# A gated recurrent layer on one core: h @ wh moved into a bf16 bank of three exact pieces

## The chip, the cores and the metric

The kernel runs on one core of a Trainium2 chip. The metric is the device time of one execution in microseconds. Every kernel is launched once per execution; a profiled execution also leaves a trace, from which all durations below are read.

## The reference

Eight sequences of 512 steps with 512 features each. The state h (8 x 512) starts at `cond_1024`. What matters of the reference:

```
def step(h, x_t):
    fused = sigmoid(concat([x_t, h]) @ w_W + w_b)
    r, z = split(fused, 2)                      # hidden_state, output_state
    memory = x_t @ wx_W + wx_b + r * (h @ wh_W + wh_b)
    h_new = z * h + (1 - z) * tanh(memory)
    return h_new, h_new
out = x + all h_new
```

Each step needs the state of the step before it. The x products (`x_t @ ...`) do not, so they can be done ahead of time. Everything is float32.

## The kernel before, in words

**Layout.** The 512 hidden units stand as 4 quarters (`k`) of 128 partitions. The state is the stationary operand of every matmul: a quarter of h, with 8 batch columns among 32 (the other 24 columns are zero; four consecutive steps, a *group* of `GS = 4`, use different rows of the same bank). The weights are streamed. Four output strips `j` of 32 PSUM partitions run side by side, so one "group of matmuls" for a quarter `k` is four matmuls with the same number of columns. The units are further cut into half A (quarters 0 and 1) and half B (2 and 3).

**Banks.** In the kernel before, each group of steps has three PSUM banks: A with 192 columns (h @ wh, z and r of half A), B with 128 (r and h @ wh of half B) and C with 64 (z of half B). `ORDER` is the order of the matmul groups in a step; the digit is the quarter of h. After them comes one portion of the x side. All matmuls are f32.

**A step after the matmuls.** DVE transposes pieces of the banks back to the layout of the state in 32 x 32 blocks (`turn_r`, `turn_h`, `turn_z`). ScalarE takes the sigmoids. A `tensor_tensor_scan` (`memory`) makes r * (h @ wh) + x part, ScalarE takes tanh, another scan (`update`) makes the new state, separately for the two quarters of each half. ScalarE copies the state into slot 0 of the state tile; GpSimd adds x for the output. The order on DVE is written out by hand: r, h, z of A, memory scans of A, r and h of B, first state scan of A, z of B, second state scan of A, memory and state scans of B.

**The x side.** The products for two groups of steps are made together from seven instead of eight half-size products (`products`, with `weight_sum` and `x_sum` making sums of weights and of x); DVE and ScalarE combine them over eight steps into the tile `xs`, from which `spread` fills the banks and `turn_x` transposes the x part of the memory.

**Order of the work.** `tc.manual_schedule()` leaves every engine's instructions in program order. PSUM, state and work tiles are double buffered or more. SP loads the weights and one chunk of x per 16 steps and stores one chunk of output per 16 steps.

**Lines.** In the profile of before, L194 is every matmul (`mm`), L224 every activation (`act`), L390 every scan, L406 the transposes of r and z, L422 that of h, L262 that of x, L558 the output adds, L534 and L495 two of the combinations of x products, L257 the `spread` copies, L232 the `seed` copy of the bias.

Of the kernel before, what the change touches and what calls it, by code (L numbers as in the profile page):

```python
# [16 lines left out]
B = 8  # L17
HU = 64

DVE_FILL = 23
IDLE = 3
LAST = 4
SYNC = mybir.DependencyInfo(mybir.DependencyClass.Sync, mybir.DependencyReason.DATA)

ORDER = "A0 B0 A1 A2 A3 B1 B2 B3 C0 C1 C2 C3"

FIRST = "A0 x A1 x A2 x A3 B0 B1 B2 B3 C0 C1 C2 C3"

BANKS = {"A": 192, "B": 128, "C": 64}

HALF = 192

WIDE = 384

SUMS = ((2,), (2,), (2, 1), (2, 1), (1,), (1, 3), (3,), (3, 3))

Q01, Q23 = slice(0, 64), slice(64, 128)

COLS = slice(64, 448)

XP = {"A": slice(0, 192), "X": slice(192, 320), "C": slice(320, 384), "B": slice(384, 512)}
# [3 lines left out]
def tile_cond_rnn_residual(  # L47
# [7 lines left out]
    wb3_d: bass.AP,  # L55
# [4 lines left out]

# [13 lines left out]

# [56 lines left out]

    wa = const.tile([P, NQ, NQ, 192], F32, name="wa")
    for k in range(NQ):
        nc.sync.dma_start(out=wa[:, k], in_=wa_d[k])
    wb = const.tile([P, NQ, NQ, 192], F32, name="wb")
    nc.sync.dma_start(out=wb[:, :3], in_=wb_d)
    nc.sync.dma_start(out=wb[:, 3], in_=wb3_d)

    def wh(bank, k, j):
        return wa[:, k, j] if bank == "A" else wb[:, k, j, {"C": slice(0, 64), "B": slice(64, 192)}[bank]]  # L140
# [3 lines left out]
    def pair(n, name, rows, slots):  # L144

        return const.tile([P, 2, rows, slots], F32, name=name).rearrange("p c n s -> p n c s")

    NH = 2 * GS  # L150
    hT = [[pair(n, f"hT{n}{i}", 32, 3) for i in range(NH)] for n in "AB"]

    md0 = [[pair(n, f"md0{n}{i}", 32, 2) for i in range(2)] for n in "AB"]
    md1 = [[pair(n, f"md1{n}{i}", 32, 2) for i in range(2)] for n in "AB"]
    hd0 = [[pair(n, f"hd0{n}{i}", B, 3) for i in range(2)] for n in "AB"]
# [11 lines left out]
    for n, t_ in enumerate(hd0[0] + hd0[1] + md0[0] + md0[1] + hT[0] + hT[1]):  # L167
        (nc.vector if n < DVE_FILL else nc.gpsimd).memset(t_, 0.0)
    for t_ in hd0[0] + hd0[1]:
        nc.gpsimd.memset(t_[:, :, :, 1], -1.0)  # L170
    idle = const.tile([P, IDLE], F32, name="idle")

    tw = [const.tile([P, 2, 2, WIDE], F32, name=f"tw{n}") for n in range(4)]
    sx = [[const.tile([P, 2, GS * B], F32, name=f"sx{n}{q}") for q in range(2)] for n in range(4)]
    step_bias = const.tile([P, HALF], F32, name="stepbias")
    xs = [const.tile([P, 512], F32, name=f"xs{n}") for n in range(2)]
    u2 = const.tile([P, WIDE], F32, name="u2")
    u3 = const.tile([P, WIDE], F32, name="u3")
    both = const.tile([P, WIDE], F32, name="both")

    def state(hf, i, slot=2):

        s = i % GS
        return hT[hf][i % NH][:, B * s : B * s + B, :, slot]

    ctx.enter_context(tc.manual_schedule())
    banks = [
        {n: psum.tile([P, w], F32, name=f"{n}{q}") for n, w in BANKS.items()}
        for q in range(2)
    ]  # L190
    xps = [psum.tile([P, 512], F32, name=f"xp{q}") for q in range(2)]

    def mm(out_, lhsT, rhs, start=False):
        nc.tensor.matmul(  # L194
            out_, lhsT, rhs, start=start, stop=False, skip_group_check=True
        )


    for t_ in list(banks[0].values()) + list(banks[1].values()):
# [10 lines left out]
    for t_ in xs:  # L210
        for c_ in (slice(0, 64), slice(448, 512)):
            nc.gpsimd.tensor_copy(t_[:, c_], bias[:, c_])
    for hf in range(2):
        for slot in (0, 2):
            nc.vector.tensor_copy(
                state(hf, 0, slot), hin[:, 2 * hf : 2 * hf + 2].rearrange("p c b -> p b c")
            )


# [9 lines left out]

    def seed(g):  # L230

        nc.scalar.copy(xps[g % 2][:, COLS], bias[:, COLS])  # L232

    def prefill(g):

        c, t0 = divmod(g * GS, TC)
        for k in range(NQ):
            for j in range(NQ):
                mm(
                    xps[g % 2][32 * j : 32 * j + 32, 64:448],  # L240
                    x_of(c, k, t0, GS),
                    wx[:, k, j, :],
                )
            yield

    def prefill_two():
        yield from prefill(2)
        yield from prefill(3)

    def source(g):  # L250

        return xs[g % 2] if g else xps[0]

    def spread(g, names):

        for n in names:
            nc.scalar.copy(banks[g % 2][n], source(g)[:, XP[n]])  # L257

    def turn_x(g, e):

        c0 = XP["X"].start + 32 * e
        nc.vector.transpose(md1[e // 2][g % 2][:, :, e % 2, 1], source(g)[:, c0 : c0 + 32])  # L262

    def wx_of(kh, nh):
        return wx[:, 2 * kh : 2 * kh + 2, 2 * nh : 2 * nh + 2]

    def x_half(o, n, kh):

        return x_of(o // 2, slice(2 * kh, 2 * kh + 2), 8 * (o % 2) + GS * n, GS)

    def weight_sum(n, k=slice(0, 2), j=slice(0, 2)):

        a, b = [
            (wx_of(0, 1), wx_of(0, 0)),
            (wx_of(1, 1), tw[0]),
            (wx_of(1, 1), wx_of(0, 1)),
            (wx_of(1, 0), tw[1]),
        ][n]
        at = (slice(0, P), k, j)
        nc.vector.tensor_tensor(tw[n][at], a[at], b[at], ALU.subtract)  # L280

    def x_sum(o, n):

        t_ = [q[o % 2] for q in sx]
        a, b, op = [
            (x_half(o, 1, 0), x_half(o, 1, 1), ALU.add),
            (t_[0], x_half(o, 0, 0), ALU.subtract),
            (x_half(o, 0, 0), x_half(o, 1, 0), ALU.subtract),
            (x_half(o, 0, 1), t_[1], ALU.subtract),
        ][n]  # L290
        nc.gpsimd.tensor_tensor(t_[n], a, b, op)

    def products(o):

        t_ = [q[o % 2] for q in sx]
        p1 = (0, x_half(o, 0, 0), wx_of(0, 0))
        p2 = (0, x_half(o, 0, 1), wx_of(1, 0))
        p3 = (0, t_[3], wx_of(1, 1))
        p4 = (1, x_half(o, 1, 1), tw[3])
        p6 = (0, t_[1], tw[1])  # L300
        p7 = (1, t_[2], tw[2])

        def pair(left, right, k, c0=0, c1=WIDE):
            for j in range(NQ):
                bank, lhs, rhs = left if j < 2 else right
                mm(
                    xps[bank][32 * j : 32 * j + 32, COLS.start + c0 : COLS.start + c1],
                    lhs[:, k],
                    rhs[:, k, j % 2, c0:c1],
                    start=right is p7 and k == 0 and j >= 2,  # L310
                )

        def shared(k):
            for j in range(NQ):
                c0 = HALF * (1 - j // 2)
                mm(
                    xps[j // 2][32 * j : 32 * j + 32, COLS.start : COLS.start + HALF],
                    t_[0][:, k],
                    tw[0][:, k, j % 2, c0 : c0 + HALF],
                )  # L320

        pair(p1, p7, 0)
        yield
        pair(p1, p7, 1)
        yield
        pair(p2, p6, 0)
        yield
        pair(p2, p6, 1)
        yield
        pair(p4, p3, 0, 0, 288)  # L330
        yield
        pair(p4, p3, 0, 288)
        shared(0)
        yield
        shared(1)
        pair(p4, p3, 1, 0, 96)
        yield
        pair(p4, p3, 1, 96)
        yield
# [7 lines left out]
    def x_side():  # L347
        for o in range(2, NG // 2):
            yield from products(o)

    seed(1)
    take(prefill(0))
    warm()
    later = x_side()
    first = {1: prefill(1), 2: prefill_two()}
    weight_sum(0)
    spread(0, "BCA")
    for e in range(NQ):
        turn_x(0, e)

    pool_done = {}
    summed = []
    for i in range(T):
# [5 lines left out]
        if t == 0:  # L369
            ot = out_p.tile([P, TC, NQ, B], F32, tag="ot", name=f"ot_{c}")  # L370

# [285 lines left out]
```

## Time and profile before

| | before |
|---|---|
| median of 3 runs | 1659.17 us (1657.54 to 1660.16) |
| span of the profiled execution | 1659.2 us |
| TensorE matmul / weight load busy | 1647.1 / 1484.3 us |
| DVE, ScalarE, GpSimd busy | 1298.5, 1106.9, 325.6 us |
| granted TensorE clock | 1.000 |
| HBM read / written | 14.70 / 8.39 MB |

How to read it: PE is TensorE's matmuls and PEld its weight loads, which overlap them; DVE is VectorE, ACT ScalarE, POOL GpSimd, SP the engine whose queue issues most DMAs. An f32 matmul appears as two records. Matmul ends are modelled, so the distance from one matmul's start to the next one's start is the safer number. In a timeline row the first column is the start in us from the start of the span, the second the length from the first start to the last end of the merged instructions, then engine, line, operation, output and input tiles, shape and count; in brackets the idle time before it and who ended it. In a row of groups the numbers behind the bar are total busy us, mean ns of one, and idle us before.

### The profile page before, as it was taken

The page shows a single profiled execution, that of the slowest core. Times are in us where ns is not written, and L with a number is a line of the kernel's source. Part 1 is how long each engine was busy: PE and PEld are TensorE (multiplying, and loading weights), DVE is VectorE, ACT ScalarE, POOL GpSimd, SP SyncE. Part 2 cuts the span into 40 slices and gives each one's busy share as a digit, 9 for nine tenths or more (in the row PEclk, how much of TensorE's full clock was granted, in tenths as well). Part 3 has the DMA queues.
Part 4 walks back from the last instruction along what each step waited for, and adds up shares of the span by engine and source line. Part 5 has one row for each costly group of instructions (what it writes and reads, how often), then busy time and mean ns, then how long its engine had stood idle before and what let it go on. Part 6 is the DMA issues. An engine that isn't in the chain of part 4 may idle for free.

```text
span 1659.2 us, 126037 instructions
## 1 busy us (share of the span) xinstructions
PE 1647.1 (99%) x54254; PEld 1484.3 (89%) x54254; DVE 1298.5 (78%) x9702; ACT 1106.9 (67%) x5884; POOL 325.6 (20%) x1284
## 2 busy tenths in 40 slices
PE   8999999999999999999999999999999999999998
PEld 5899999999999888899999999988899999999997
DVE  6877777777777777777777777777777777777776
ACT  4666666666666666666666666666666666666665
POOL 2221121211211212112112121121121211211211
PEclk9999999999999999999999999999999999999999
DMA  4000000000000000000000000000000000000000
GB/s 180 17 5 18 17 18 18 17 6 18 17 17 18 5 18 18 18 18 5 18 18 18 18 12 10 18 17 18 18 5 18 17 18 18 5 17 11 11 11 10
DMA packets 11512, 31.16 MB, mean 19 GB/s; under 512 B 1220, under 2 KB 1732, under 8 KB 10824
## 3 DMA queue, kind: packets, MB, share of 16 engines
q1 hardware_dynamic: 10800, 22.94, 4.0%
q8 instruction: 424, 6.95, 1.8%
q14 instruction: 136, 1.11, 0.2%
q10 hardware_dynamic: 152, 0.16, 0.0%
HBM read 14.70 MB, written 8.39 MB: 14 GB/s over the span
## 4 chain that ended last, share of the span: by engine, by line
PE 98%; DMA 1%; DVE 1%; issue 0%; ACT 0%; SPq 0%
PE A L194 40%; PE B L194 26%; PE xp L194 18%; PE C L194 13%; DMA wb<-in_wb_dram 1%; DMA wx<-in_wx_dram 0%; DVE tr L406 0%; DVE m L390 0%; DVE tz L406 0%; DVE hTA L390 0%; DVE md1A L422 0%; DVE md1B L422 0%; ACT hTB L224 0%; SPq L130 0%; DVE hTB L390 0%
## 5 line engine op out<-in xcount | busy, mean ns | idle before, releaser
L194 PE MATMUL A<-wa,hTA 128*32 128x192 f32 x8176 | 555.5, 327 | 2.7 <-DVE hTA L390 2.7
L194 PE MATMUL B<-wb,hTA 128*32 128x128 f32 x8192 | 453.0, 273 | 0.9 <-DMA wb<-in_wb_dram 0.9
L194 PE MATMUL A<-wa,hTB 128*32 128x192 f32 x8176 | 446.6, 326 | 0.0
L194 PEld LDWEIGHTS A<-wa,hTA 128*32 128x32 f32 x8176 | 290.7, 122 | 128.4 <-DVE hTA L390 107.1
L558 POOL TENSOR_TENSOR ot<-xin,hTB 128x16 f32<-128x16 f32 x503 | 125.6, 250 | 1292.4 <-DVE hTB L390 1281.8
L194 PEld LDWEIGHTS B<-wb,hTA 128*32 128x32 f32 x8192 | 346.8, 122 | 10.8 <-DMA wb<-in_wb_dram 1.3
L194 PE MATMUL B<-wb,hTB 128*32 128x128 f32 x8192 | 338.6, 273 | 0.1
L194 PEld LDWEIGHTS A<-wa,hTB 128*32 128x32 f32 x8176 | 324.3, 122 | 15.5 <-DVE hTB L390 0.3
L224 ACT ACTIVATE md0A<-tr 128x16 f32<-128x16 f32 x512 | 112.3, 219 | 314.4 <-DVE tr L406 314.4
L406 DVE STREAM_TRANSPOSE tr<-A 128x64 f32<-128x64 f32 x511 | 127.7, 250 | 214.3 <-PE A L194 199.3
L194 PE MATMUL xp<-tw,sx 128*32 128x384 f32 x1984 | 274.2, 406 | 0.3 <-issue 0.3
L194 PEld LDWEIGHTS B<-wb,hTB 128*32 128x32 f32 x8192 | 261.1, 122 | 0.4 <-DMA wb<-in_wb_dram 0.4
L390 DVE TENSOR_TENSOR_SCAN hTB<-hd0B,hTB 128x24 f32<-128x24 f32 x1024 | 157.8, 195 | 100.5 <-ACT hTB L224 100.5
L194 PE MATMUL C<-wb,hTB 128*32 128x64 f32 x8192 | 230.0, 219 | 0.1
L194 PE MATMUL C<-wb,hTA 128*32 128x64 f32 x8192 | 229.1, 219 | 0.0
L194 PE MATMUL xp<-wx,xin 128*32 128x384 f32 x1056 | 210.1, 486 | 0.0
L194 PEld LDWEIGHTS C<-wb,hTA 128*32 128x32 f32 x8192 | 206.6, 122 | 0.0
L390 DVE TENSOR_TENSOR_SCAN hTA<-hd0A,hTA 128x24 f32<-128x24 f32 x1024 | 190.9, 186 | 0.0
L194 PEld LDWEIGHTS C<-wb,hTB 128*32 128x32 f32 x8192 | 179.5, 122 | 0.6 <-issue 0.4
L224 ACT ACTIVATE hd0B<-tz 128x16 f32<-128x16 f32 x512 | 115.7, 226 | 94.8 <-DVE tz L406 94.8
L224 ACT ACTIVATE hTB<-hTB 128x16 f32<-128x16 f32 x512 | 120.1, 235 | 79.2 <-DVE hTB L390 70.3
L224 ACT ACTIVATE hTA<-m 128x8 f32<-128x8 f32 x1024 | 160.8, 206 | 2.5
(98 smaller groups left out, 2710.0 us busy)
## 6 DMA issues: line engine op xcount, KB each, us to landing
xin<-in_x_dram SPq DMA_DIRECT2D x31, 256.0 KB, 3.3
out_dram<-ot SPq DMA_DIRECT2D x31, 256.0 KB, 2.1
wx<-in_wx_dram SPq DMA_DIRECT2D x4, 768.0 KB, 7.1
wa<-in_wa_dram SPq DMA_DIRECT2D x4, 384.0 KB, 9.1
wb<-in_wb_dram SPq DMA_DIRECT2D x1, 1152.0 KB
wb<-in_wb_dram SPq DMA_DIRECT2D x1, 384.0 KB, 11.2
out_dram<-ot SPq DMA_DIRECT2D x1, 192.0 KB, 2.1
head<-in_xh_dram ACTq DMA_DIRECT2D x1, 144.0 KB, 5.0
```

What stands on the lines that cost most here:

```text
L194: nc.tensor.matmul(out_, lhsT, rhs, start=start, stop=False, skip_group_check=True)
L224: inst = nc.scalar.activation(out_, in_, func, **kw).ins
L390: return nc.vector.tensor_tensor_scan(*[t_[:, :, c_].rearrange("p n c s -> p (n c s)") for t_ in (out_, d0, d1)], 0.0, ALU.mult, ALU.add,).ins
L406: inst = nc.vector.transpose(t_.rearrange("p c n -> p (c n)"), raw[n][hf]).ins
L558: return engine.tensor_tensor(ot[:, t, 2 * hf : 2 * hf + 2, :].rearrange("p c n -> p n c"), x_of(c, slice(2 * hf, 2 * hf + 2), t, 1).rearr ...
```

## The change

**h @ wh leaves the f32 banks.** Banks A and B now hold only z and r of their half, 128 columns each in f32. h @ wh of *both* halves goes to a bank of its own, `hbanks` (H, 128 columns, double buffered by step), as bf16 matmuls. To be exact, the state is cut into three bf16 numbers (`pieces`) and the weights into three (`whp`, made once by `split`). The three pieces of the state stand as 24 stationary columns; the three pieces of the weights are streamed one after the other, so each quarter of h takes three groups of bf16 matmuls. The 24 result rows and a row block that holds the bias are summed by the memory scan itself, which now runs over `SL = 5` slots (`turn_h` transposes the H bank into slots 0 to 3; the x part is slot 4).

**Making the pieces.** After half hf's state scans, `grown(hf)` issues: on ScalarE `first_piece` (a copy of the f32 state, whose upper 16 bits are read as bf16), on GpSimd `other_pieces` (two subtractions) and `again` (the copy of the state to slot 0, which was on ScalarE).

**The orders.** `ORDER` becomes `A0 A1 B0 B1 A2 A3 H0 H1 H2 H3 B2 B3`, then one portion of x. r and z of a half are transposed in one operation (`turn_gates`). DVE's order in a step is written out below; each `memory` and `update` is one scan.

**The x side** is plain: one product of 384 columns per quarter, `prefill`, a quarter in every step, two groups ahead; no sums, no combinations, no `xs`. The first two groups are prefilled before the first step.

Core of the diff:

```diff
-ORDER = "A0 B0 A1 A2 A3 B1 B2 B3 C0 C1 C2 C3"
-BANKS = {"A": 192, "B": 128, "C": 64}
+NP = 3
+SL = 5
+ROWS = NP * B
+ORDER = "A0 A1 B0 B1 A2 A3 H0 H1 H2 H3 B2 B3"
...
+    def first_piece(hf, i):
+        act(("p", hf, i % 2), pieces[hf][i % 2][:, :, :B], state(hf, i), AF.Copy)
+
+    def other_pieces(hf, i):
+        t_ = pieces[hf][i % 2]
+        hi = t_.bitcast(BF16)[:, :, 1::2]
+        nc.gpsimd.tensor_tensor(t_[:, :, B : 2 * B], state(hf, i), high(hf, i), ALU.subtract)
+        nc.gpsimd.tensor_tensor(
+            t_[:, :, 2 * B : 3 * B], t_[:, :, B : 2 * B], hi[:, :, B : 2 * B], ALU.subtract
+        )
+
+    def again(hf, i):
+        nc.gpsimd.tensor_copy(state(hf, i, 0), state(hf, i))
...
+    def split(k):
+        w = whf[:, k]
+        t_ = work.tile([P, NQ, 2 * HU], F32, tag="split", name=f"split{k}")
+        nc.scalar.copy(whp[:, k, :, 0], w)
+        nc.vector.tensor_tensor(t_, w, whp[:, k, :, 0], ALU.subtract)
+        nc.scalar.copy(whp[:, k, :, 1], t_)
+        nc.vector.tensor_tensor(whp[:, k, :, 2], t_, whp[:, k, :, 1], ALU.subtract)
...
+            else:
+                to = hbanks[i % 2]
+                hs = pieces[k // 2][i % 2].bitcast(BF16)[:, k % 2, 1 : 2 * ROWS : 2]
+                for p in range(NP):
+                    for j in range(NQ):
+                        mm(to[32 * j : 32 * j + ROWS, :], hs, whp[:, k, j, p], start=k == p == 0)
+        if g in later:
+            take(later[g], 1)
...
+        def turn_gates(hf):
+            t_ = work.tile([P, 4, 32], F32, tag=f"t{hf}", name=f"t{hf}_{i}")
+            nc.vector.transpose(t_.rearrange("p c n -> p (c n)"), ps["AB"[hf]])
+            tz[hf] = t_
+            act(("r", hf, g % 2, s), md0[g % 2][:, 2 * hf : 2 * hf + 2, rows, SL - 1], t_[:, 2:, rows], AF.Sigmoid)
+            act(("zc", hf, i % 2), hd0[hf][i % 2][:, :, :, 2], t_[:, :2, rows], AF.Sigmoid, scale=-1.0)
...
+        def turn_h():
+            nc.vector.transpose(
+                md1[g % 2][:, :, rows, : SL - 1].rearrange("p c n s -> p c s n"), hbanks[i % 2]
+            )
...
+        def memory(hf, q):
+            scan(ms[hf][:, q], md0[g % 2][:, 2 * hf + q, rows], md1[g % 2][:, 2 * hf + q, rows])
+            act(("n", hf, q, i % 8), state(hf, i, 1)[:, q], ms[hf][:, q, :, SL - 1], AF.Tanh)
...
-        turn_r(0)
-        turn_h(0)
-        turn_z(0)
-        memory(0, 0)
-        memory(0, 1)
-        turn_r(1)
-        turn_h(1)
-        update(0, 0)
-        turn_z(1)
-        tc.add_manual_dep(update(0, 1), r_done[1].name, SYNC)
+        turn_gates(0)
+        turn_h()
+        memory(0, 0)
+        memory(0, 1)
+        update(0, 0)
+        update(0, 1)
+        turn_gates(1)
+        grown(0)
         memory(1, 0)
         memory(1, 1)
         update(1, 0)
         update(1, 1)
+        grown(1)
...
+        if s == 0 and g + 1 < NG:
+            turn_x(g + 1)
+        if s in (1, 2) and g + 1 < NG:
+            spread(g + 1, "AB"[s - 1])
+        for hf in range(2):
+            add(hf, t, 1, nc.gpsimd if i < T - 1 else nc.vector)
```

More of the change, by code (lines that the diff above doesn't have):

```diff
@@ L54, in tile_cond_rnn_residual @@
     wb_d: bass.AP,
-    wb3_d: bass.AP,
+    wh_d: bass.AP,
     bias_d: bass.AP,
@@ L130, in tile_cond_rnn_residual @@
         nc.sync.dma_start(out=wx[:, k], in_=wx_d[k])
-    wa = const.tile([P, NQ, NQ, 192], F32, name="wa")
+    whf = const.tile([P, NQ, NQ, 128], F32, name="whf")
     for k in range(NQ):
[L134 to L140, printed above, removed]
@@ L142, in tile_cond_rnn_residual @@
-    load_x(0, 1)
[L144 to L155, printed above, removed]
+        nc.sync.dma_start(out=whf[:, k], in_=wh_d[k])
@@ new lines, in tile_of, with cells, state, high @@
+    def tile_of(hf, i):
+        q, s = i // GS % 2, i % GS
+        return hT[hf][q], 192 * s
+    def cells(hf, i):
+        t_, at = tile_of(hf, i)
+        return t_[:, at : at + 192].rearrange("p (c n s) -> p c n s", c=2, n=32)
+    def state(hf, i, slot=2):
+        s = i % GS
+        return cells(hf, i)[:, :, B * s : B * s + B, slot]
+    def high(hf, i):
+        t_, at = tile_of(hf, i)
+        s = i % GS
+        v = t_[:, at : at + 192].bitcast(BF16).rearrange("p (c n s) -> p c n s", c=2, n=32)
+        return v[:, :, B * s : B * s + B, 5]
@@ L166, in tile_cond_rnn_residual @@
     nc.scalar.activation(const.tile([P, 1], F32, name="table"), zeros[:, :1], AF.Sigmoid)
-    for n, t_ in enumerate(hd0[0] + hd0[1] + md0[0] + md0[1] + hT[0] + hT[1]):
-        (nc.vector if n < DVE_FILL else nc.gpsimd).memset(t_, 0.0)
     for t_ in hd0[0] + hd0[1]:
+        nc.gpsimd.memset(t_, 0.0)
         nc.gpsimd.memset(t_[:, :, :, 1], -1.0)
[L171 to L184, printed above, removed]
+    for t_ in md0:
+        nc.gpsimd.memset(t_, 1.0)
+        nc.gpsimd.memset(t_[:, :, :, 0], 0.0)
+    for t_ in md1 + pieces[0] + pieces[1] + hT[0] + hT[1]:
+        nc.vector.memset(t_, 0.0)
     ctx.enter_context(tc.manual_schedule())
[L187 to L190, printed above, removed]
+    banks = [{n: psum.tile([P, 128], F32, name=f"{n}{q}") for n in "AB"} for q in range(2)]
+    hbanks = [psum.tile([P, 2 * HU], F32, name=f"H{q}") for q in range(2)]
     xps = [psum.tile([P, 512], F32, name=f"xp{q}") for q in range(2)]
     def mm(out_, lhsT, rhs, start=False):
[L194 to L199, printed above, removed]
+        nc.tensor.matmul(out_, lhsT, rhs, start=start, stop=False, skip_group_check=True)
+    for t_ in list(banks[0].values()) + list(banks[1].values()) + hbanks:
         mm(t_, none, none[:, :1].broadcast_to([P, t_.shape[1]]), start=True)
@@ L209, in tile_cond_rnn_residual @@
     nc.vector.tensor_copy(bias, xps[0])
[L210 to L217, printed above, removed]
+    for t_ in hbanks:
+        nc.vector.tensor_copy(t_, bias[:, 384:])
     written = {}
@@ L228, in act @@
         return inst
+    def first_piece(hf, i):
[10 more added lines that the diff above has]
+    for hf in range(2):
+        nc.vector.tensor_copy(state(hf, 0), hin[:, 2 * hf : 2 * hf + 2])
+        first_piece(hf, 0)
+        other_pieces(hf, 0)
+        again(hf, 0)
     def seed(g):
-        nc.scalar.copy(xps[g % 2][:, COLS], bias[:, COLS])
+        nc.scalar.copy(xps[g % 2][:, :384], bias[:, :384])
     def prefill(g):
@@ L238, in prefill @@
             for j in range(NQ):
[L239 to L243, printed above, removed]
-            yield
[L246 to L339, printed above, removed]
@@ L341, in take, with spread, turn_x @@
+                mm(xps[g % 2][32 * j : 32 * j + 32, :384], x_of(c, k, t0, GS), wx[:, k, j, :])
+            yield
+    def spread(g, n):
+        nc.scalar.copy(banks[g % 2][n], xps[g % 2][:, {"A": XA, "B": XB}[n]])
+    def turn_x(g):
+        nc.vector.transpose(md1[g % 2][:, :, :, SL - 1], xps[g % 2][:, XX])
     def take(it, n=None):
@@ L345, in take @@
             n = None if n is None else n - 1
-    def x_side():
-        for o in range(2, NG // 2):
-            yield from products(o)
-    seed(1)
[L352 to L362, printed above, removed]
+    def split(k):
[5 more added lines that the diff above has]
+        nc.vector.tensor_tensor(whp[:, k, :, 2], t_, whp[:, k, :, 1], ALU.subtract)
+    seed(0)
+    take(prefill(0))
+    seed(1)
+    take(prefill(1))
+    spread(0, "A")
+    spread(0, "B")
+    turn_x(0)
+    for k in range(NQ):
+        split(k)
+    later = {}
     for i in range(T):
@@ L370, in tile_cond_rnn_residual @@
             ot = out_p.tile([P, TC, NQ, B], F32, tag="ot", name=f"ot_{c}")
-        for n in (ORDER if i else FIRST).split():
-            if n == "x":
-                take(first[1], 1)
-                continue
+        if s == 0 and g + 2 < NG:
+            later[g] = prefill(g + 2)
+            seed(g + 2)
+        for n in ORDER.split():
             bank, k = n[0], int(n[1])
-            hs = hT[k // 2][i % NH][:, :, k % 2, 2]
-            for j in range(NQ):
-                to = ps[bank] if i or bank != "A" else xps[0][:, XP["A"]]
-                mm(to[32 * j : 32 * j + 32, :], hs, wh(bank, k, j))
@@ L381, in tile_cond_rnn_residual @@
-        if 1 <= i < 4:
-            take(first[2], 2 if i == 3 else 3)
-        else:
-            take(later if i else first[1], 1)
+            if bank in "AB":
+                w = (wa if bank == "A" else wb)[:, k]
+                hs = cells(k // 2, i)[:, k % 2, :, 2]
+                for j in range(NQ):
+                    mm(ps[bank][32 * j : 32 * j + 32, :], hs, w[:, j])
+            else:
+                to = hbanks[i % 2]
+                hs = pieces[k // 2][i % 2].bitcast(BF16)[:, k % 2, 1 : 2 * ROWS : 2]
+                for p in range(NP):
+                    for j in range(NQ):
+                        mm(to[32 * j : 32 * j + ROWS, :], hs, whp[:, k, j, p], start=k == p == 0)
@@ L447, in memory @@
+        def turn_h():
+            nc.vector.transpose(
+                md1[g % 2][:, :, rows, : SL - 1].rearrange("p c n s -> p c s n"), hbanks[i % 2]
+            )
+        ms = [work.tile([P, 2, B, SL], F32, tag=f"m{hf}", name=f"m{hf}_{i}") for hf in range(2)]
         def memory(hf, q):
-            c_ = slice(q, q + 1)
-            scan(c_, ms[hf], md0[hf][g % 2][:, rows], md1[hf][g % 2][:, rows])
-            act(("n", hf, q, i % NH), state(hf, i, 1)[:, :, c_], ms[hf][:, :, c_, 1], AF.Tanh)
+            scan(ms[hf][:, q], md0[g % 2][:, 2 * hf + q, rows], md1[g % 2][:, 2 * hf + q, rows])
+            act(("n", hf, q, i % 8), state(hf, i, 1)[:, q], ms[hf][:, q, :, SL - 1], AF.Tanh)
@@ L453, in update, with grown @@
         def update(hf, q):
             s1 = (i + 1) % GS
-            new = hT[hf][(i + 1) % NH][:, B * s1 : B * s1 + B]
-            return scan(slice(q, q + 1), new, hd0[hf][i % 2], hT[hf][i % NH][:, rows])
-        turn_r(0)
-        turn_h(0)
-        turn_z(0)
+            new = cells(hf, i + 1)[:, q, B * s1 : B * s1 + B]
+            scan(new, hd0[hf][i % 2][:, q], cells(hf, i)[:, q, rows])
+        def grown(hf):
+            if i < T - 1:
+                first_piece(hf, i + 1)
+                other_pieces(hf, i + 1)
+                again(hf, i + 1)
@@ L481, in tile_cond_rnn_residual @@
         update(1, 1)
-        for hf in range(2):
-            act(("h", hf, (i + 1) % NH), state(hf, i + 1, 0), state(hf, i + 1), AF.Copy)
+        grown(1)
         if i < 3:
             load_x(i + 1)
-        o, u = divmod(i, 2 * GS)
-        nxt, two = o + 1 < NG // 2, o + 2 < NG // 2
-        if i == 0:
-            nc.scalar.copy(xs[1][:, COLS], xps[1][:, COLS])
-            spread(1, "B")
-            turn_x(1, 0)
-        add_ = nc.vector.tensor_tensor
-        if u == 3 and o and nxt:
-            add_(xs[0][Q23, COLS], xps[0][Q23, COLS], both[Q23], ALU.add)
-        elif u == 7 and two:
-            nc.vector.tensor_copy(xs[0][Q01, COLS], xps[0][Q01, COLS])
-        elif u == 0 and o and nxt:
-            add_(u3[Q23], xps[1][Q23, COLS], u2[Q23], ALU.add)
@@ L548, in tile_cond_rnn_residual @@
-        if i < len(SUMS):
-            for n in SUMS[i]:
-                weight_sum(n, *divmod(summed.count(n), 2))
-                summed.append(n)
-        if i == 4:
-            for to, c_ in ((Q01, slice(256, 448)), (Q23, slice(64, 256))):
-                nc.vector.tensor_tensor(step_bias[to], bias[Q23, c_], bias[Q01, c_], ALU.subtract)
-        for n in range(IDLE - 1):
-            nc.vector.memset(idle[:, n : n + 1], 0.0)
-        def add(hf, engine):
-            return engine.tensor_tensor(
-                ot[:, t, 2 * hf : 2 * hf + 2, :].rearrange("p c n -> p n c"),
-                x_of(c, slice(2 * hf, 2 * hf + 2), t, 1).rearrange("p c n -> p n c"),
-                state(hf, i + 1),
-                ALU.add,
-            ).ins
@@ L584, in tile_cond_rnn_residual @@
+        if s in (1, 2) and g + 1 < NG:
+            spread(g + 1, "AB"[s - 1])
+        for hf in range(2):
+            add(hf, t, 1, nc.gpsimd if i < T - 1 else nc.vector)
+        if t == TC - 1:
+            nc.sync.dma_start(out=out[c], in_=ot.rearrange("p t k b -> p (t k b)"))
             xins.pop(c)
```

166 lines of the change are left out of this document (29 added, 137 removed).

## The prediction

> **What bounds the kernel now.** I read the page first, then the granted clock, then the timeline of one step in the middle and of the steps near the end.
>
> ```profile
> span 1659.2 us, 126037 instructions
> PE 1647.1 (99%) x54254; PEld 1484.3 (89%) x54254; DVE 1298.5 (78%) x9702; ACT 1106.9 (67%) x5884; POOL 325.6 (20%) x1284
> ...
> PE 98%; DMA 1%; DVE 1%; issue 0%; ACT 0%; SPq 0%
> ```
>
> TensorE is busy 99% of the span and carries 98% of the chain that ended last. The profiled span, 1659.2 us, equals the median of the runs (1659.17), so a sum made against it needs no correction. A step in the middle, TensorE alone (start, modelled duration):
>
> ```profile
> 803.71 0.54 PE L194 MATMUL A<-wa,hTA 128*32 128x192 f32 x8
> ...
> 804.57 0.86 PE L194 MATMUL A<-wa,hTB 128*32 128x192 f32 x16
> 805.22 0.43 PE L194 MATMUL B<-wb,hTA 128*32 128x128 f32 x8
> ...
> 805.88 0.43 PE L194 MATMUL C<-wb,hTA 128*32 128x64 f32 x16
> ...
> 806.33 0.49 PE L194 MATMUL xp<-wx,xin 128*32 128x384 f32 x2
> ...
> 806.97 0.54 PE L194 MATMUL A<-wa,hTA 128*32 128x192 f32 x8
> ```
>
> The starts follow each other without a hole. A group is four matmuls side by side in the four column strips (eight records, since an f32 matmul runs as two passes). The starts give, per group: 0.32 us for 192 columns (804.57 to 805.22 is two), 0.22 for 128 (three from 805.22 to 805.88), 0.11 for 64 (four from 805.88 to 806.33), 0.64 for 384. So the time is columns times a constant, and the step is full.
>
> Beside it runs a loop: state, matmuls, transposes, sigmoid, scan, tanh, scan, state. Near the end the x matmuls have run out, and there this loop shows:
>
> ```profile
> 1648.02 0.25 DVE L406 STREAM_TRANSPOSE tr<-A 128x64 f32<-128x64 f32 x1 [0.94 <-PE A L194]
> ...
> 1648.30 0.22 ACT L224 ACTIVATE md0A<-tr 128x16 f32<-128x16 f32 x1 [0.97 <-DVE tr L406]
> ...
> 1648.56 0.28 DVE L390 TENSOR_TENSOR_SCAN m<-md0A,md1A 128x16 f32<-128x16 f32 x2
> ...
> 1648.78 0.31 ACT L224 ACTIVATE hTA<-m 128x8 f32<-128x8 f32 x2
> ...
> 1649.03 0.20 DVE L390 TENSOR_TENSOR_SCAN hTA<-hd0A,hTA 128x24 f32<-128x24 f32 x1
> ...
> 1649.29 0.55 PE L194 MATMUL A<-wa,hTA 128*32 128x192 f32 x8 [0.24 <-DVE hTA L390]
> 1649.30 0.17 DVE L390 TENSOR_TENSOR_SCAN hTA<-hd0A,hTA 128x24 f32<-128x24 f32 x1
> 1649.39 0.25 DVE L390 TENSOR_TENSOR_SCAN m<-md0B,md1B 128x16 f32<-128x16 f32 x2
> ...
> 1650.85 0.40 PE L194 MATMUL B<-wb,hTA 128*32 128x128 f32 x8
> ...
> 1651.10 0.25 DVE L406 STREAM_TRANSPOSE tr<-A 128x64 f32<-128x64 f32 x1 [0.94 <-PE A L194]
> ```
>
> From these starts come the hand-offs used below, each from start to start with the waiting in it: transpose to sigmoid 0.28, sigmoid to scan 0.26, scan to tanh 0.22, tanh to state scan 0.25, state scan to the matmul that loads it 0.26, last matmul's successor (1650.85) to the transpose of its bank 0.25. A scan is followed 0.09 later by the next DVE operation. This loop of half A takes 3.08 us a step. In mid-kernel the step is 3.20 (from 20.21, below, to 1649.29 over 509 steps), so the kernel is TensorE-bound with the loop only just underneath. That is the fact on which the change turns.
>
> **TensorE's work after the change.** The h columns leave the f32 banks: 4 groups of 128 columns, 4 x 0.22 = 0.88 us less per step. They return as 12 bf16 groups (4 quarters of h by 3 pieces of the weights) of 128 columns with one pass each. No such matmul is in the trace; the nearest row is C's f32 group of 64 columns, whose two passes take 0.11 us, 0.055 a pass, with as many weight loads and matmuls per pass (four and four) as a bf16 group. At 0.055 the H bank costs 0.66. I take that; the bounds are 0.64 (pure column rate) and twice it. The x side loses its factored products: plain, it is 0.64 a step in place of 7/8 of that, +0.08. Sum: -0.88 + 0.66 + 0.08 = -0.14 us of TensorE work per step, from 3.20 to 3.06. If TensorE stayed the bound that would be 70 us gained.
>
> **It does not stay the bound.** The new order on TensorE is A0 A1 B0 B1 A2 A3 H0 H1 H2 H3 B2 B3 x. A0 to B1 need half A's new state, A2 and A3 half B's. Bank H serves both halves, ends with half B's state, and both memory scans read it. DVE's queue, in order, is: transpose A, transpose H, two memory scans and two state scans of half A, transpose B, two memory scans and two state scans of half B. So half B's transpose stands behind half A's last state scan, which waits for tanh. Before, the two halves were interleaved: r and h of B were transposed between A's memory scan and A's state scan. After, they run one behind the other, and the loop goes through both.
>
> The new operations are sized from these rows:
>
> ```profile
> L406 DVE STREAM_TRANSPOSE tr<-A 128x64 f32<-128x64 f32 x511 | 127.7, 250 | 214.3 <-PE A L194 199.3
> L422 DVE STREAM_TRANSPOSE md1A<-A 128x64 f32<-128x64 f32 x511 | 107.7, 211 | 0.0
> L262 DVE STREAM_TRANSPOSE md1A<-xp 128x32 f32<-128x32 f32 x2 | 0.3, 198 | 2.2 <-ACT A L257 2.2
> L390 DVE TENSOR_TENSOR_SCAN m<-md0A,md1A 128x16 f32<-128x16 f32 x1024 | 142.2, 181 | 8.3
> L390 DVE TENSOR_TENSOR_SCAN hTA<-hd0A,hTA 128x24 f32<-128x24 f32 x1024 | 190.9, 186 | 0.0
> ```
>
> A transpose of 128 columns is in no row. From 32 to 64 columns the duration rises 13 to 52 ns, so 64 more columns add 0.03 to 0.10; the other bound is two transposes of 64 in a row (+0.17). I take +0.07: 0.35 from its start to the sigmoid. Transpose H to memory scan is a hand-off inside DVE; no row shows it, I take the same, rounded up, 0.36. A memory scan of 40 elements in place of 16: 5 ns for 8 elements by the rows, up to 0.05 for all 24; I take +0.04, so 0.26 to tanh.
>
> The loop, from the end of H3's streaming (0):
> - transpose H starts 0.25; memory scan A 0.61; tanh 0.87; first state scan of A 1.12; its second 1.26 (its tanh comes 0.11 later, plus the longer scan).
> - transpose B 1.36 (its own matmuls B2 B3 end at 0.44, transposable at 0.69: it waits for the queue alone); sigmoid of r 1.71; memory scan B 1.97; tanh 2.23; state scan of B 2.48; A2 on TensorE 2.74.
> - A2 A3 0.44 and the H bank 0.66, with 0.03 for the restart (1649.29 to the next group in the trace is 0.36 against 0.32): 1.13. The loop closes at 3.87 us.
>
> On the way TensorE has B2 B3 x (1.08) until A0 may start at 1.38, then A0 A1 B0 B1 (0.88) until 2.26, and waits for A2 until 2.74: about 0.3 and 0.5 us of waiting per step, where before it had nearly none.
>
> Two side chains must be weighed, since GpSimd now makes the second and third piece of the state. The rows:
>
> ```profile
> 807.71 0.25 POOL L558 TENSOR_TENSOR ot<-xin,hTB 128x16 f32<-128x16 f32 x1 [2.57 <-DVE hTB L390]
> 807.75 0.62 DVE L534 TENSOR_TENSOR xs<-u,both 64x384 f32<-64x384 f32 x1
> 807.91 0.56 POOL L558 TENSOR_TENSOR ot<-xin,hTA 128x16 f32<-128x16 f32 x1
> ```
>
> (a) H2 needs half B's pieces. From the end of B's second state scan (2.81): two GpSimd subtractions of 0.25 with 0.05 to 0.08 at each of three hand-offs, about 3.5. TensorE reaches H2 at 2.74 + 0.03 + 0.44 + 0.33 = 3.54. Hidden, with no margin; each 0.05 longer costs 0.05 a step. ScalarE's first piece, 0.23, is shorter than this. (b) Half A's subtractions and state copy run on GpSimd from 1.53 to 2.3, over memory scan B at 1.97. The second add above lasts 0.56 in place of 0.25 and ends 0.1 after the DVE operation that it overlaps, which has both inputs in SBUF and is 67 ns longer than its PSUM-reading siblings (617 against 550). A scan also reads two SBUF tiles, so it may be held. I take those 67 ns, 0.07; the bounds are nothing and one whole GpSimd operation, 0.25. The Trainium skill (SBUF — State Buffer, section Who interferes with whom) says that a DVE instruction with two SBUF inputs and a GpSimd one that reads SBUF exclude each other for the whole instruction; by that rule the price is up to 0.25 a step and the total some 90 us above mine. The second add above agrees with that rule.
>
> Other edits cost nothing on this path: turn of x, spread and seed lie behind half B's last scan, in the 0.9 us until transpose A; the copy of the state to slot 0 moves from ScalarE to GpSimd and is needed a step later; the combining of factored products on DVE and ScalarE, which filled gaps, is gone. The first piece of A stands on ScalarE behind both sigmoids of B and before B's tanh: it starts at 1.93 and the next one is free by 2.05, before 2.23.
>
> Pitch: 3.87 + 0.07 = 3.94 us. Start and end:
>
> ```profile
> 8.65 0.48 ACT L232 COPY xp<-bias 128x384 f32<-128x384 f32 x1 [4.62 <-DVE bias L209]
> ...
> 11.35 0.85 PE L194 MATMUL xp<-wx,head 128*32 128x384 f32 x8 [0.53 <-DMA wx<-in_wx_dram]
> ...
> 20.21 0.51 PE L194 MATMUL A<-wa,hTA 128*32 128x192 f32 x8
> ...
> 1655.99 0.31 DVE L390 TENSOR_TENSOR_SCAN hTB<-hd0B,hTB 128x24 f32<-128x24 f32 x2 [0.19 <-ACT hTB L224]
> ...
> 1656.62 0.33 SPq L568 DMA_DIRECT2D out_dram<-ot  x1
> ```
>
> Two prefills of 2.6 us now precede the loop; the last wx arrives at 11.35, so they end near 14.5. Then the weights are split: per quarter two ScalarE copies and two DVE subtractions of 512 columns, some 0.6 each by the 0.48 for 384, partly one behind the other: 2 us, 8 for four. The first transpose H comes near 23 (20 to 26). The last needs 2.6 to the end of B's last scan and 2.9 from there to the end of the span (1656.3 to 1659.2). Total: 23 + 511 x 3.94 + 5.5 = 2042, stated as 2040.
>
> **Rivals.**
> - Faster: the loop hides and TensorE stays the bound. For this, the stretch from H3's end to A2, 2.74, must fit under B2 B3 x A0 A1 B0 B1, 0.44 + 0.64 + 0.88 = 1.96. Then 28 + 511 x 3.06 = 1592. For it: TensorE's work falls. Against it: transpose B alone, behind A's scans, makes 0.35 + 0.26 + 0.26 + 0.25 + 0.26 of serial work after 1.36. Even with 3.19 a step, where it only breaks even, the loop would have to be 0.75 shorter. Chance 0.06.
> - GpSimd decides: its pieces come late or hold the scans, by the whole 0.25: 4.19 a step, 28 + 511 x 4.19 = 2170. For it: no margin in (a). Chance 0.17.
> - bf16 groups do not run at C's rate but at half of it: H 1.32, all of it on the loop: 4.60 a step, 2380. Against it: C's passes. Chance 0.05.
> - The waits throttle TensorE to half clock, so that the 1.13 on the loop doubles: 5.07, 2620. Against it: in the last steps TensorE waits 0.24 in each and the granted clock (the column after POOL's) stays 1.00:
>
> ```profile
> 1590.00:1650.00 60.00, 57.58 (x1936) 51.73 (x1931) 45.03 (x355) 38.20 (x213) 10.24 (x42) 1.00 0.04 13
> ```
>
>   Chance 0.03. The Trainium skill (TensorE: Matmul & The Clock Gate, section A second HAM failure mode) tells of short idle times between groups that made the clock swing; this row does not show it.
> - The rest, 0.04: hand-offs much shorter than these rows, ending around the old time.
>
> **How the numbers follow.** The forecast as counted has 0.65. With GpSimd's rival that is 0.82, which the range holds. Its low end: both long transposes at the small bound, scans no longer than now, no holding: 3.71 a step, 1925. Its high end: both transposes as two in a row (+0.2), GpSimd's 0.25, 0.05 for (a): 4.37, 2260. Faster by over 0.2% (about what a measurement of this kernel can tell from no change): 0.06 and a part of the rest, 0.07; within it 0.01; slower 0.92.
>
> **What would show it.** Right: TensorE's busy share near 80%, waits of A's weight loads on half B's state scan near 0.5 us a step and on half A's near 0.3, transpose B starting right behind half A's second state scan, a pitch near 3.94, DVE and ScalarE less busy than before. Wrong: no waits on TensorE with a pitch of 3.06; H groups of over 0.06 each; H2's weight load waiting on GpSimd; a memory scan B that starts late, at the end of a GpSimd operation; a clock under 1.

## The result, and the profile after

The changed kernel takes 2171.62 us, median of 4 runs (2171.10 to 2172.81); the kernel before 1659.66, median of 4 runs. The ratio is 1.3086, 95% interval 1.3067 to 1.3104: 512 us slower, where 381 were forecast. The forecast loop is there; two of its hand-offs were sized too small.

The page of the changed kernel:

```profile
span 2169.3 us, 142668 instructions
PE 1808.5 (83%) x61452; PEld 1312.2 (60%) x61452; DVE 1246.9 (57%) x5793; ACT 972.5 (45%) x5514; POOL 781.7 (36%) x4110
...
DVE 40%; PE 32%; ACT 16%; issue 9%; DVEq 1%; DMA 1%; POOL 0%; POOLq 0%
```

Against the same lines of before: no engine is full any more, and the chain that ended last, 98% TensorE before, now goes round DVE, TensorE and ScalarE. That is what a latency loop looks like. GpSimd's busy time more than doubled, and it is not on the chain.

One step of the changed kernel, from the timeline of all engines (here `t<-A`, `t<-B` are the transposes of z and r, `md<-H` the transpose of the H bank, `m` the memory scans; `pcA` and `pcB` are the pieces of the state; a merged row x2 is the scans or tanhs of the two quarters):

```profile
1001.09 0.62 PE L148 MATMUL B<-wb,hTB 128*32 128x128 f32 x16
...
1001.31 0.42 DVE L279 STREAM_TRANSPOSE md<-H 128x128 f32<-128x128 f32 x1 [0.33 <-PE H L148]
...
1001.52 0.83 PE L148 MATMUL xp<-wx,xin 128*32 128x384 f32 x8
1001.83 0.37 DVE L265 TENSOR_TENSOR_SCAN m<-md,md 128x40 f32<-128x40 f32 x2
1002.11 0.35 ACT L167 ACTIVATE hTA<-m 128x8 f32<-128x8 f32 x2 [0.76 <-DVE m L265]
1002.43 0.31 DVE L265 TENSOR_TENSOR_SCAN hTA<-hd0A,hTA 128x24 f32<-128x24 f32 x2 [0.22 <-ACT hTA L167]
1002.65 0.29 DVE L273 STREAM_TRANSPOSE t<-B 128x128 f32<-128x128 f32 x1
...
1002.69 0.66 PE L148 MATMUL A<-wa,hTA 128*32 128x128 f32 x16 [0.34 <-DVE hTA L265]
...
1002.98 0.23 ACT L167 ACTIVATE md<-t 128x16 f32<-128x16 f32 x1 [0.52 <-DVE t L273]
...
1003.17 0.62 PE L148 MATMUL B<-wb,hTA 128*32 128x128 f32 x16
1003.17 0.21 POOL L180 TENSOR_TENSOR pcA<-pcA 128x16 f32<-128x16 f32 x1
...
1003.24 0.39 DVE L265 TENSOR_TENSOR_SCAN m<-md,md 128x40 f32<-128x40 f32 x2 [0.30 <-ACT md L167]
1003.33 0.21 POOL L185 COPY hTA<-hTA 128x16 f32<-128x16 f32 x1
1003.52 0.36 ACT L167 ACTIVATE hTB<-m 128x8 f32<-128x8 f32 x2
1003.84 0.31 DVE L265 TENSOR_TENSOR_SCAN hTB<-hd0B,hTB 128x24 f32<-128x24 f32 x2 [0.21 <-ACT hTB L167]
...
1004.10 0.66 PE L148 MATMUL A<-wa,hTB 128*32 128x128 f32 x16 [0.31 <-DVE hTB L265]
...
1004.58 0.52 PE L148 MATMUL H<-whp,pcA 128*24 128x128 bf16 x24
...
1005.25 0.62 PE L148 MATMUL B<-wb,hTB 128*32 128x128 f32 x16
```

Follow the DVE rows: half B's transpose (1002.65) starts right behind half A's state scans, although its bank has been ready for about a microsecond; only then come B's sigmoid, memory scan, tanh and state scan, and A2 at 1004.10. TensorE waits twice, in front of A0 (x ends near 1002.16, A0 starts at 1002.69) and of A2 (B1 ends near 1003.61): about 0.5 us each, counted from the starts. The brackets say 0.34 and 0.31, since they count from the modelled ends. From the end of one H bank (1001.09) to the next (1005.25) are 4.16 us.

### The profile page after: what moved, and what is told of

Same layout as the page of the kernel before. It is cut to its first block, busy times and chain, and to the rows that moved or that the text cites. A ratio compares the mean times of both kernels' runs of the same rounds, so it can differ in the third digit from the quotient of the medians.

```text
span 2169.3 us, 142668 instructions
## 1 busy us (share of the span) xinstructions
PE 1808.5 (83%) x61452; PEld 1312.2 (60%) x61452; DVE 1246.9 (57%) x5793; ACT 972.5 (45%) x5514; POOL 781.7 (36%) x4110
## 4 chain that ended last, share of the span: by engine, by line
DVE 40%; PE 32%; ACT 16%; issue 9%; DVEq 1%; DMA 1%; POOL 0%; POOLq 0%
PE H L148 16%; PE A L148 15%; DVE m L265 12%; DVE md L279 10%; DVE hTA L265 7%; ACT md L167 6%; ACT hTA L167 5%; ACT hTB L167 5%; DVE hTB L265 5%; DVE t L273 5%; DVEq L265 1%; DMA whf<-in_wh_dram 0%; DMA xin<-in_x_dram 0%; DMA head<-in_xh_dram 0%; DVE split L219 0%
## 5 line engine op out<-in xcount | busy, mean ns | idle before, releaser
L265 DVE TENSOR_TENSOR_SCAN m<-md,md 128x40 f32<-128x40 f32 x2048 | 391.5, 232 | 207.8 <-ACT md L167 153.1
L148 PE MATMUL A<-wa,hTA 128*32 128x128 f32 x8192 | 339.2, 283 | 183.4 <-DVE hTA L265 183.4
L167 ACT ACTIVATE md<-t 128x16 f32<-128x16 f32 x1024 | 238.4, 233 | 542.6 <-DVE t L273 542.4
L148 PE MATMUL A<-wa,hTB 128*32 128x128 f32 x8192 | 338.6, 283 | 163.1 <-DVE hTB L265 163.1
L148 PE MATMUL xp<-wx,xin 128*32 128x384 f32 x4032 | 418.3, 487 | 0.0
L148 PEld LDWEIGHTS A<-wa,hTB 128*32 128x32 f32 x8192 | 206.8, 125 | 295.1 <-DVE hTB L265 295.1
L279 DVE STREAM_TRANSPOSE md<-H 128x128 f32<-128x128 f32 x512 | 216.6, 423 | 169.2 <-PE H L148 169.1
L148 PE MATMUL H<-whp,pcB 128*24 128x128 bf16 x12288 | 266.2, 219 | 3.1 <-ACT whp L220 1.9
L148 PE MATMUL H<-whp,pcA 128*24 128x128 bf16 x12288 | 265.9, 219 | 0.7 <-DVE whp L221 0.5
L148 PEld LDWEIGHTS <-pcA 128*24 128x24 bf16 x12288 | 228.4, 93 | 1.1 <-issue 1.1
L167 ACT ACTIVATE hTB<-m 128x8 f32<-128x8 f32 x1024 | 186.3, 218 | 54.4 <-DVE m L265 0.2
```

Of the source, the lines that this page charges most:

```text
L148: nc.tensor.matmul(out_, lhsT, rhs, start=start, stop=False, skip_group_check=True)
L167: inst = nc.scalar.activation(out_, in_, func, **kw).ins
L265: return nc.vector.tensor_tensor_scan(*[t_.rearrange("p n s -> p (n s)") for t_ in (out_, d0, d1)], 0.0, ALU.mult, ALU.add).ins
L279: nc.vector.transpose(md1[g % 2][:, :, rows, : SL - 1].rearrange("p c n s -> p c s n"), hbanks[i % 2])
```

## The experiments

In each the changed kernel is the base, unless said otherwise. The theory: one serial loop through both halves, closed by DVE's queue order. The rivals: GpSimd, and TensorE's own work. The experiments ran in several rounds, and the median of the kernel before lay between 1660.20 and 1663.03 us in them, so differences of some 3 us are not resolved.

**1. Half B's transpose early.**

```diff
+        turn_gates(1)
         update(0, 0)
         update(0, 1)
-        turn_gates(1)
         grown(0)
```

> The changed kernel with one edit: half B's transpose of r and z (with its two sigmoids) is issued on DVE and ScalarE before half A's two state scans in place of after them. Theory (one serial loop through both halves, closed by DVE's queue order; hand-offs as in the changed kernel's trace): transpose B can then start about 1.0 us after the end of the H bank in place of 1.55, memory scan B at 1.6, A2 at 2.48, pitch 3.63 in place of 4.16 us; 511 x 0.53 = 271 us less, about 1900 us. Rival 1 (GpSimd holds the scans or delays the pieces and sets the pitch): little change, 2100 to 2171. Rival 2 (TensorE's own work sets it): no change, 2171.

Measured: 1912.94 us, ratio to the kernel before 1.1496 (1.1475 to 1.1516): 259 us less, half of the whole loss, for one line moved in a queue. TensorE's timeline:

```profile
1014.35 0.63 PE L148 MATMUL B<-wb,hTB 128*32 128x128 f32 x16
...
1015.96 0.66 PE L148 MATMUL A<-wa,hTA 128*32 128x128 f32 x16 [0.34 <-DVE hTA L265]
1016.44 0.62 PE L148 MATMUL B<-wb,hTA 128*32 128x128 f32 x16
1016.88 0.63 PE L148 MATMUL A<-wa,hTB 128*32 128x128 f32 x16
...
1017.99 0.64 PE L148 MATMUL B<-wb,hTB 128*32 128x128 f32 x16
...
1019.59 0.66 PE L148 MATMUL A<-wa,hTA 128*32 128x128 f32 x16 [0.32 <-DVE hTA L265]
```

The pitch is 3.63, as worked out, and the wait in front of A2 is gone. Both rivals fall. But the path is another one than the expectation had: A0 starts 1.61 after the end of the H bank (1014.35 to 1015.96), and A0 A1 B0 B1 A2 A3 and the H bank, 2.03 (to 1017.99), follow without a hole. So half A's path now sets the pitch. Half B's state scan starts 0.30 before A2, where the hand-off needs 0.26: half B's path, from which the 3.63 was worked out, is 0.04 shorter, and that both give nearly the same number is luck. The 13 us above the expected 1900 lie in longer steps (3.71 to 3.79, with an H bank that takes 0.75 to 0.81 in place of 0.67, at a granted clock of 1.00); what stretches those is open.

**2. No x matmuls** (their share is missing from the result).

```diff
-        if g in later:
-            take(later[g], 1)
```

> The changed kernel without its x matmuls after the first two groups of steps (their products are left out of the result; everything else is issued). Theory: the 0.64 us of x matmuls per step lie wholly beside the loop, in front of A0's wait; that wait grows by as much and the time stays, 2165 to 2175. Rival (TensorE's work sets the pitch): 511 x 0.64 less, 1845. Rival (idle TensorE gets half the clock): slower, by up to 1.1 us a step, 2700.

Measured: 2166.04 us. 0.64 us of TensorE work per step taken away, 324 in all by TensorE's busy time (1808.5 to 1484.6), gave 6. TensorE's wait in front of A0 grew from 0.34 to 0.98:

```profile
1000.84 0.66 PE L148 MATMUL A<-wa,hTA 128*32 128x128 f32 x16 [0.98 <-DVE hTA L263]
```

So the return from the factored to the plain x side, 0.08 us of TensorE a step, costs nothing here either. The granted clock stayed at 0.997 with TensorE at 69%: these waits did not lower it.

**3. The state scans wait for ScalarE alone.** The copy to slot 0 goes to ScalarE; the wait on old output adds goes to the transpose of A.

```diff
-        nc.gpsimd.tensor_copy(state(hf, i, 0), state(hf, i))
+        act(("h", hf, i % 8), state(hf, i, 0), state(hf, i), AF.Copy)
...
+            if hf == 0 and i - 7 in pool_done:
+                tc.add_manual_dep(inst, pool_done[i - 7].name, SYNC)
...
```

> The changed kernel with the state scans' wait on GpSimd taken away: the copy of the state into slot 0 goes from GpSimd to ScalarE, behind the first piece, and the wait for GpSimd's old output adds goes to the transpose of A, which has time. Theory: the 0.32 us from a tanh to its state scan (0.25 before the change) is the price of a second semaphore to wait for; it falls back to 0.25 in both halves, 511 x 0.14 = 70 us less, 2100. Rival 1 (the 0.07 come from the tanh itself or its strided operands): no change, 2171. Rival 2 (GpSimd's operations hold scans for a whole operation): one GpSimd operation fewer beside memory scan B, up to 511 x 0.2 less, 2070.

Measured: 2114.50 us, 57 less (0.11 a step).

```profile
1000.79 0.35 ACT L169 ACTIVATE hTA<-m 128x8 f32<-128x8 f32 x2 [0.69 <-DVE m L268]
1001.04 0.34 DVE L268 TENSOR_TENSOR_SCAN hTA<-hd0A,hTA 128x24 f32<-128x24 f32 x2 [0.15 <-ACT hTA L169]
1001.30 0.29 DVE L276 STREAM_TRANSPOSE t<-B 128x128 f32<-128x128 f32 x1
```

Tanh to state scan is 0.25 again, as in the kernel before, in place of 0.32. The wait on GpSimd was long satisfied (its copy of the state ends about 3 us before the scan that needs it); what cost was that there were two. The transpose of A, which took over a wait on GpSimd, starts 0.33 after the first matmul of the H bank in place of 0.25; that lies off the loop. Of the 0.14, about 0.04 are given back: the second state scan now waits for its own tanh, and transpose B follows the first scan after 0.26 in place of 0.22. The slot-0 copy also left GpSimd here, but experiment 5 shows that GpSimd's load next to the scans has no price.

**4. The H transpose writes neighbours** (the pieces then stand in wrong slots of the sum).

```diff
-                md1[g % 2][:, :, rows, : SL - 1].rearrange("p c n s -> p c s n"), hbanks[i % 2]
+                md1[g % 2][:, :, rows].rearrange("p c n s -> p c (n s)")[:, :, : 4 * B], hbanks[i % 2]
```

> The changed kernel with the transpose of the H bank writing 32 neighbouring numbers for each of the four blocks, in place of numbers 20 bytes apart; same tile, same readers. The pieces then lie in the wrong slots of the sum. Theory: the 423 ns of that transpose against 317 for the equally large one of bank A come from the spacing of what it writes; it falls to about 317, the pitch by 0.11, the time to about 2117. Rival (the longer time comes from the H bank or from a slower start after the wait on TensorE): no change, 2171.

Measured: 2116.25 us, 55 less. The groups of DVE, first of the changed kernel, then of this one (busy us, mean ns, idle before):

```profile
L279 DVE STREAM_TRANSPOSE md<-H 128x128 f32<-128x128 f32 x512 | 216.6, 423 | 169.2 <-PE H L148 169.1
```

```profile
L279 DVE STREAM_TRANSPOSE md<-H 128x128 f32<-128x128 f32 x512 | 162.3, 317 | 169.2 <-PE H L148 169.2
L273 DVE STREAM_TRANSPOSE t<-A 128x128 f32<-128x128 f32 x512 | 162.2, 317 | 308.5 <-PE A L148 308.3
```

106 ns a step times 511 are 54 us. The spacing of the writes, 20 bytes, is the whole difference. The Trainium skill (SBUF — State Buffer, section Specifications (TRN2)) says that SBUF lines are 16 bytes and that each crossing to a new line pays; these two rows agree.

**5. No subtractions on GpSimd in the loop** (the second and third piece of the state stay those of the first step).

```diff
                 first_piece(hf, i + 1)
-                other_pieces(hf, i + 1)
```

> The changed kernel without GpSimd's two subtractions per half in the loop (the second and third piece of the state stay as they were at the first step). Theory: they lie beside the loop, half A's with time to spare and half B's just in time; 0 to 0.03 us a step, 2155 to 2171. Rival (the time of 2170 that was worked out beforehand for GpSimd holding memory scan B or bringing the pieces late by 0.25 a step is the true cause): 511 x 0.25 less, about 2045.

Measured: 2168.25 us, 3 less. GpSimd's subtractions neither hold the scans nor bring the pieces late. The 2170 us that the prediction worked out for that rival agree with the measured time by chance.

**6. One weight piece of three** (so h @ wh is inexact).

```diff
-                for p in range(NP):
+                for p in range(1):
```

> The changed kernel with only the first of the three pieces of the weights streamed: 4 bf16 groups per step in the H bank in place of 12. Theory: the H bank lies whole on the loop at 0.055 us a group, 0.44 less; but H2 needs half B's pieces from GpSimd, which come 1.05 us after half B's first state scan starts, and this wait takes over: H ends at 1.05 + 0.11 after that scan in place of 1.41, 0.25 a step less, about 2045 us, with TensorE's weight loads of half B's pieces waiting for GpSimd. Rival 1 (no such side chain): the whole 0.44, 1947. Rival 2 (TensorE's matmuls of H are hidden): no change, 2171.

Measured: 2032.87 us, 139 less, 0.27 a step. The H bank is on the loop, and when it is shortened by 0.44, GpSimd's chain for half B's pieces takes over, as the waits show (us in total, times, longest):

```profile
PEld L148 <- POOL pcB L180: 84.8, 509, 0.5
```

That is 0.17 a step, and 0.44 - 0.17 is the 0.27 gained. With four bf16 groups fewer ahead of it, H2 comes 0.22 sooner and waits 0.17, so in the changed kernel this chain is hidden by only some 0.05.

**7. Experiments 1 and 3 together.**

> Both edits together: half B's transpose of r and z ahead of half A's state scans, and the state scans without a wait on GpSimd. Theory: the savings add, as both shorten the same loop, less 0.06 that half A's state scan no longer has on the way to memory scan B: transposes B at 1.0, sigmoid 1.33, memory scan B 1.61, tanh 1.89, state scan 2.14, A2 2.40, pitch 3.55, about 1860 us. It stays above the 1660 of the kernel before, since TensorE's work is 3.06 and the loop 3.55. Rival (another chain, GpSimd's pieces for H2, takes over): no less than the first edit alone gives.

Measured: 1899.94 us, ratio to the kernel before 1.1438 (1.1415 to 1.1461): 13 less than experiment 1, where 53 were expected. The steady pitch is 3.60:

```profile
1003.59 0.66 PE L150 MATMUL A<-wa,hTA 128*32 128x128 f32 x16 [0.28 <-DVE hTA L268]
...
1007.20 0.66 PE L150 MATMUL A<-wa,hTA 128*32 128x128 f32 x16 [0.27 <-DVE hTA L268]
```

As in experiment 1, TensorE waits in front of A0 and hardly ever for half B's state, for which the weight loads of the changed kernel waited 295.1 us (us in total, times, longest):

```profile
PE A L150 <- DVE hTA L268: 140.1, 484, 0.9
PEld A L150 <- DVE hTB L268: 3.6, 14, 0.4
```

So half A's path sets the pitch here too, and of the two second waits only half A's lies on it. A0 starts 1.54 after the end of the H bank in place of 1.61, but the matmuls from A0 to the end of the H bank take 2.06 in place of 2.03: 3.60.

**8. In addition B1 behind the H bank**, to see what took over in 7.

```diff
-ORDER = "A0 A1 B0 B1 A2 A3 H0 H1 H2 H3 B2 B3"
+ORDER = "A0 A1 B0 A2 A3 H0 H1 H2 H3 B1 B2 B3"
```

> The kernel with both edits (half B's transpose early, no wait on GpSimd), and in addition B1 moved behind the H bank in TensorE's order: A0 A1 B0 A2 A3 H0 H1 H2 H3 B1 B2 B3. Theory: with both edits the steady step is 3.60 and not the 3.55 forecast because half A's own loop took over: A0 starts 1.54 after the end of H, and A0 A1 B0 B1 A2 A3 H, 2.06 of TensorE's work, follow without a hole. With B1 behind H, A2 need not stand behind it; half B's state becomes the bound at 2.40, TensorE waits for it 0.1 to 0.2 again, pitch 3.55: 511 x 0.05 = 25 us less than with both edits, 1875. Rival (half B's loop is the bound already, or the H bank waits for GpSimd's pieces): no change, 1900.

Measured: 1903.19 us, ratio 1.1454 (1.1435 to 1.1473): no change. B1 no longer stands in front of A2, and the pitch is 3.61 all the same, since A2 now waits for half B's state:

```profile
1005.71 0.66 PE L150 MATMUL A<-wa,hTA 128*32 128x128 f32 x16
...
1005.80 0.38 DVE L268 TENSOR_TENSOR_SCAN m<-md,md 128x40 f32<-128x40 f32 x2
1005.88 0.23 ACT L169 ACTIVATE pcA<-hTA 128x16 f32<-128x16 f32 x1
...
1006.01 0.21 ACT L169 ACTIVATE hTA<-hTA 128x16 f32<-128x16 f32 x1
...
1006.13 0.31 ACT L169 ACTIVATE hTB<-m 128x8 f32<-128x8 f32 x2
...
1006.36 0.31 DVE L268 TENSOR_TENSOR_SCAN hTB<-hd0B,hTB 128x24 f32<-128x24 f32 x2 [0.19 <-ACT hTB L169]
...
1006.62 0.66 PE L150 MATMUL A<-wa,hTB 128*32 128x128 f32 x16
...
1009.32 0.66 PE L150 MATMUL A<-wa,hTA 128*32 128x128 f32 x16
```

B0, which starts at 1006.18, ends near 1006.40; A2 starts at 1006.62, the usual 0.26 after half B's state scan. So in experiment 7 the two paths were equally long, and shortening one alone gains nothing: the expectation was right that half A's path had taken over, and wrong that half B's is shorter. Half B's has grown: memory scan B to its tanh is 0.33, in experiment 1 it was 0.27. The slot-0 copy, now on ScalarE, stands in the queue right before half B's tanh, which starts with no idle time before it. In experiment 3 the same copy had time. The rest of the shortfall of 7 lies in longer single steps, not explained. No version tried reaches the kernel before.

## Why the prediction was right, point by point

**The bound.** Right: the serial loop replaced TensorE. Experiment 2 shows that the x matmuls in front of TensorE's wait are free, experiment 1 that the place of half B's transpose in DVE's queue is the largest of the terms tried.

**TensorE's work.** Right in the number, and by luck as far as the rows of before go: the H bank takes 0.67 (1004.58 to 1005.25) where 0.66 was taken from C's passes. But a pass of C has 64 columns and a bf16 group 128. By the prediction's own rows 128 f32 columns take 0.22 in two passes, 0.11 a pass, and twelve groups at that would be the 1.32 of the rival with a chance of 0.05; no row of before shows a faster bf16 pass, nor the bound of 0.64. The measured 0.056 a group shows it: 128 bf16 columns go through in half the time of a pass of 128 f32 columns. With that the rival fell.

**The loop's length.** The step that was mis-sized: 3.94 forecast, 4.16 measured. Term by term: H transpose to memory scan 0.36, measured 0.52. Of this 0.11 is the write spacing (experiment 4), for which the rows of before gave nothing and the bounds allowed "two transposes of 64 in a row"; the other 0.05 is the hand-off inside DVE, 0.10 from the transpose's end (1001.73) to the scan. Tanh to state scan 0.25, measured 0.32, in both halves, +0.14: the prediction noted that the slot-0 copy moves to GpSimd, and asked only whether it would be late, not whether the second wait has a price (experiment 3). Memory scan to tanh 0.28 in place of 0.26, twice, +0.04. The others came out 0.07 shorter together, the matmul stretch 0.02 longer. 3.87 + 0.16 + 0.14 + 0.04 - 0.07 + 0.02 = 4.16. The mean over the run is 4.19, as some steps are 0.36 longer; in one of them the memory scan starts 0.46 after the H transpose with nothing else in its way in the trace, and that is not explained. The forecast came this near with the help of 0.07 that does not exist (next point): the loop itself was 0.29 short.

**Holding by GpSimd, +0.07.** Wrong, it is nothing: sigmoid to memory scan B is 0.26 with GpSimd's subtraction and copy beside it, and memory scan to tanh 0.28 in both halves. The exclusion that the prediction cites from the Trainium skill does not measurably delay these scans. The prediction also counted its GpSimd rival too high: 4.19 adds the whole 0.25 to a pitch that already holds 0.07 of it; for the holding alone it would be 4.12, some 2133 us.

**Side chain (a).** Right: hidden, with some 0.05 to spare (experiment 6), where 0.04 was worked out.

**Start and end.** The first transpose H starts at 24.26 (23 forecast), the span ends 6.2 after the last one (5.5).

**The signs.** The waits on TensorE came at both places named, near 0.5 us each, where 0.3 and 0.5 were given (by the idle time before A's weight loads, the column that was named, 1.05 on half A's state and 0.58 on half B's); TensorE is at 83% (near 80), DVE and ScalarE are less busy. The clock stayed at 0.998. The faster rival fell because no step came near 3.19 us.

## What to carry to other kernels

Where a recurrence sits just under the bound of a full engine, work taken from that engine is worth nothing unless the recurrence gets shorter too: trace the loop through every in-order queue, and ask of each instruction on it whether the one ahead of it waits for something else. An operation whose bank is ready belongs ahead of one that waits; here that is half of the loss. When sizing the loop, count the spacing of writes and the number of semaphores that an instruction on it waits for, even those long satisfied.

## What the runs showed of the hardware that was not expected

Writing 20 bytes apart costs a 128 x 128 transpose 106 ns (423 against 317). A second, long satisfied wait costs a state scan 0.07 us. A bf16 group of 128 columns takes 0.056 us, half of an f32 pass of as many columns. At the start TensorE's clock did fall, though none of its waits between 17 and 24 us was over 1.0 us. Stretches of the changed kernel (us, busy of PE, PEld, DVE, ACT, POOL, then granted clock, DMA share, GB/s):

```profile
22.00:24.00 2.00, 0.55 (x16) 0.27 (x17) 1.31 (x3) 1.00 (x2) 0.00 (x0) 1.00 0.00 0
24.00:26.00 2.00, 2.00 (x36) 0.98 (x39) 1.46 (x7) 0.73 (x5) 0.20 (x1) 0.63 0.00 0
26.00:28.00 2.00, 2.00 (x45) 2.00 (x41) 0.99 (x5) 0.96 (x6) 1.13 (x8) 0.52 0.03 8
28.00:30.00 2.00, 2.00 (x84) 1.34 (x75) 1.11 (x4) 0.54 (x4) 0.22 (x2) 1.00 0.00 0
```

While the H bank waited for the split weights TensorE was busy about a quarter of the time, and the next four microseconds ran at little over half clock. In the loop, with TensorE 69 to 83% busy and waits of 0.3 to 1.0 us by the profile, it did not happen.
